# Turning a causal attention's exponentials on VectorE and through DRAM instead of on TensorE

## The chip, the core and the metric

The kernel runs on one core of a Trainium2 chip. Five engines work beside each other, each through its own instructions in a fixed order, and wait for one another by semaphores: TensorE (PE; its weight loads are listed apart as PEld), VectorE (DVE), ScalarE (ACT), GpSimd (POOL), and SyncE (SP), which here only issues DMA transfers. The metric is the time of one execution on the device in microseconds (us); lower is better. All data is float32.

## The reference

Two decoder layers work on x of shape (8, 128, 512): 8 batches of 128 tokens of 512 features. Each of six sublayers is added to x and followed by a layer norm. Layer 0 has a causal attention, an autocorrelation with a context of the same shape, and a gated sum of low-rank experts. Layer 1 has a causal attention with normalized queries and keys and a slope per head, a cross attention, and a low-rank feed-forward. The change is in the two causal attentions, which have 32 heads of 16 features:

```python
scores = jnp.einsum('bhqd,bhkd->bhqk', q, k) / math.sqrt(hd)
scores = jnp.where(causal, scores, -jnp.inf)
att = jax.nn.softmax(scores, axis=-1)
out = jnp.einsum('bhqk,bhkd->bhqd', att, v)
return out.transpose(0, 2, 1, 3).reshape(b, l, d) @ Wo.T + bo
```

Layer 1 clips queries, keys and values to ±8, normalizes queries and keys over all 512 features, and adds slope x (k − q) to the scores before the softmax.

## The kernel before

**A step.** Both attentions go through `Heads16`, which treats 16 pairs of (head, half of the partitions) at once; one such round is called a step. Layer 0 has 16 steps: four pairs of batches (p), and for each four groups of eight heads (f), where the two units of a step are the two batches of the pair. Layer 1 has 16 steps too: eight batches (b), each with f = 0 and f = 2, where the two units are two groups of eight heads. The loops are at lines 516 to 547 and 847 to 897.

A causal mask lets the first 64 queries see only the first 64 keys. So scores are held in two parts: late queries by 128 keys (part 0, two heads x), and early queries by 64 keys (part 1). A step's exponentials are 128 partitions (64 queries of each unit) by 4 rows r by 384 columns.

**What a step does.** The constructor (lines 158 to 187) makes the scores on PE into two pairs of PSUM banks, then on DVE adds the mask or the slopes and takes the minimum of the negated sums, 16 pieces in all (L184), into the tile `e`, which has two buffers. `exps` (L197) makes the exponentials on ACT in place, with their sums. `turn` (lines 213 to 238) transposes `e` on PE, twelve 128x128 blocks into PSUM (L228), since the product with the values needs keys on the partitions; DVE copies the first half to `pT` and ACT the second (L229). `out` multiplies with the values on PE (lines 240 to 257).

The division by the sums differs. In layer 1 `divide` (lines 202 to 211) takes reciprocals on DVE and multiplies the exponentials on POOL, two instructions for each half, before the turn. In layer 0 the reciprocals are spread over 16 features on POOL (L221), turned on PE by two more transposes (L236) and multiplied to the output (L261).

**Order.** In the step n after its scores: the first half of the exponentials, `out` of step n−2, the next step's queries and keys (layer 0) or the next batch's (layer 1), `turn` of step n−1, the second half of the exponentials, and a projection of an earlier pair or batch. Beside layer 0's steps 7 to 15 run pieces of the autocorrelation of the first four batches (`beside`, lines 498 to 508), with much work on DVE in `chosen` (lines 427 to 451).

In layer 1 the queries of batch b+1 are made and normalized in batch b's first step (`normed`, lines 656 to 677; the normalization itself is L667 on DVE), transposed on PE in its second step (`turned_queries`, L691). The keys are normalized in the second step between the two halves of the scores (`between`, lines 174 to 177), transposed (L701) and multiplied with two masks on DVE (L703). The residual's layer norm is made a step later by `catch_up` (lines 117 to 121).

The order in which each engine gets its instructions is not the order of the program text alone. A planner takes them by their place in the text and by when it reckons that their inputs are there, then fixes one list for each engine. `tc.issue_after(x)` holds the instructions inside it behind instruction x on x's engine. A tile of a pool with k buffers waits until the user of the same buffer k tiles before is done. SP's DMA transfers are such a list too: one that waits holds those behind it.

## Time and profile before

| | us |
|---|---|
| median of three runs (lowest to highest) | 883.1 (881.8 to 883.6) |
| the profiled execution | 883.9 |
| its span, first to last instruction | 882.1 |
| layer 0, steps 8 to 14 (91.3 to 198.3 of the span) | 107.0 |
| layer 1, steps 16 to 19 (322.7 to 371.6) | 48.9 |
| layer 1, steps 20 to 29 (371.6 to 481.9) | 110.3 |
| layer 1, from the scores of step 30 to the last projection's end (481.9 to 510.5) | 28.6 |

Layer 0's steps 8 to 14 take 12.4, 16.2, 17.0, 15.8, 12.4, 16.3 and 16.9 us. A batch of layer 1 in its steady part takes 22.1 us.

How to read the profile's lines: a line of a group gives the line of the kernel, the engine, the operation, the output and input tiles, the count, then busy time and the mean of one instruction in ns, and then how long the engine stood idle just before them and what ended that. A line of the DMA issues gives count, size of one and the median time from issue to landing. In the chain of work that ended last each piece has its start, the time that it holds on the chain, and the engine, tile and line. The granted clock of PE is 0.994 of full over the span.

### The profile page before, as it was taken

The page shows a single profiled execution, that of the slowest core. Times are in us where ns is not written, and L with a number is a line of the kernel's source. Part 1 is how long each engine was busy: PE and PEld are TensorE (multiplying, and loading weights), DVE is VectorE, ACT ScalarE, POOL GpSimd, SP SyncE. Part 2 cuts the span into 40 slices and gives each one's busy share as a digit, 9 for nine tenths or more (in the row PEclk, how much of TensorE's full clock was granted, in tenths as well). Part 3 has the DMA queues.
Part 4 walks back from the last instruction along what each step waited for, and adds up shares of the span by engine and source line. Part 5 has one row for each costly group of instructions (what it writes and reads, how often), then busy time and mean ns, then how long its engine had stood idle before and what let it go on. Part 6 is the DMA issues. An engine that isn't in the chain of part 4 may idle for free.

```text
span 882.1 us, 17898 instructions
## 1 busy us (share of the span) xinstructions
PE 853.1 (97%) x6482; PEld 529.9 (60%) x6482; DVE 545.8 (62%) x2166; ACT 369.3 (42%) x1535; POOL 188.5 (21%) x267
## 2 busy tenths in 40 slices
PE   9999999999899999999999999999999999999996
PEld 5766655655455455555555687758475846576454
DVE  3656787777869567777778622735363545467654
ACT  3877564754222136666666503213122322224310
POOL 2500223133333314555555300000000000000000
PEclk9999999999999999999999999999999999999999
DMA  8700000130300002000004010331213211313340
GB/s 327 306 2 26 1 14 13 49 108 1 144 13 24 1 1 97 2 1 2 2 2 145 27 72 1 75 88 42 48 37 85 44 47 37 83 43 76 81 97 36
DMA packets 30073, 50.73 MB, mean 58 GB/s; under 512 B 5536, under 2 KB 22048, under 8 KB 28192
## 3 DMA queue, kind: packets, MB, share of 16 engines
q1 hardware_dynamic: 27424, 47.49, 17.9%
q10 hardware_dynamic: 2560, 2.10, 1.1%
q8 instruction: 51, 0.84, 0.4%
q14 instruction: 38, 0.31, 0.1%
HBM read 30.69 MB, written 2.10 MB: 37 GB/s over the span
## 4 chain that ended last, share of the span: by engine, by line
PE 72%; DVE 17%; ACT 6%; POOL 2%; issue 1%; DMA 1%; SPq 0%; ACTq 0%; POOLq 0%; DVEq 0%
PE pqx L86 9%; PE pox L994 7%; PE pv L86 5%; PE pkx L86 4%; PE pvx L86 4%; PE s_x L932 4%; PE o_x L977 4%; PE pq L86 4%; PE pk L86 3%; PE po L711 3%; ACT e_a L197 3%; DVE e_a L184 3%; PE pt_a L228 3%; PE pof L618 2%; PE s_a L165 2%; PE po L86 2%
## 5 line engine op out<-in xcount | busy, mean ns | idle before, releaser
L197 ACT ACTIVATE e_a<-e_a,m_a 128x128 f32<-128x128 f32 (+1 forms) x512 | 184.8, 365 | 100.2 <-DVE m_a L184 100.2
L953 ACT ACTIVATE e_x<-s_x,m_x 128x256 f32<-128x256 f32 x128 | 58.6, 483 | 140.0 <-DVE m_x L943 132.1
L197 ACT ACTIVATION_READ_ACCUMULATOR e_a<-e_a,m_a 128x1 f32 x512 | 97.6, 191 | 0.0
L86 PE MATMUL pqx<-xTx,w_X_q 128*128 128x256 f32 x384 | 84.9, 380 | 0.0
L86 PEld LDWEIGHTS pqx<-xTx,w_X_q 128*128 128x128 f32 x384 | 72.6, 190 | 11.4 <-issue 1.8
L994 PE MATMUL pox<-w_X_o,oTx 128*128 128x512 f32 x168 | 74.1, 596 | 0.7 <-DVE oTx L983 0.6
L942 DVE TENSOR_REDUCE m_x<-s_x 128x4 f32<-128x1024 f32 x32 | 37.6, 1218 | 41.2 <-PE s_x L932 41.2
L97 POOL TENSOR_TENSOR rs_x<-ve_x,neghalf 128x1 f32<-128x1 f32 x7 | 3.8, 548 | 268.8 <-DVE ve_x L95 249.8
L211 POOL TENSOR_TENSOR e_a<-e_a,rc_a 128x512 f32<-128x512 f32 (+1 forms) x64 | 52.7, 845 | 34.9 <-DVE rc_a L208 19.3
L994 PEld LDWEIGHTS pox<-w_X_o,oTx 128*128 128x128 f32 x168 | 31.3, 190 | 40.9 <-issue 39.2
L932 PE MATMUL s_x<-kTx,qTx 32*128 32x256 f32 x768 | 50.0, 385 | 1.2 <-ACT e_x L953 1.1
L228 PE MATMUL pt_a<-ident,e_a 128*128 128x128 f32 x384 | 48.0, 273 | 2.7 <-DVE m_a L184 2.7
L228 PEld LDWEIGHTS pt_a<-ident,e_a 128*128 128x128 f32 x384 | 43.6, 140 | 11.1 <-issue 5.0
L184 DVE CUSTOM_DVE_ANT_0 e_a<-s_a,masks 128x128 f32<-128x128 f32 (+1 forms) x256 | 47.1, 252 | 4.5 <-PE s_a L165 3.2
L932 PEld LDWEIGHTS s_x<-kTx,qTx 32*128 32x128 f32 x768 | 39.0, 184 | 17.4 <-issue 11.7
L184 DVE CUSTOM_DVE_ANT_0 e_a<-s_a,alibi 128x128 f32<-128x128 f32 (+1 forms) x256 | 47.4, 253 | 2.2 <-PE s_a L165 1.3
L977 PE MATMUL o_x<-pT_x,vx 128*32 128x512 f32 x384 | 43.7, 595 | 1.9 <-issue 0.7
L184 DVE DVE_READ_ACCUMULATOR2_ANT m_a<- 128x1 f32 x512 | 42.4, 83 | 0.1
L961 DVE STREAM_TRANSPOSE e_x<-e_x 128x1024 f32<-128x1024 f32 x32 | 39.7, 1241 | 0.8
L960 DVE TENSOR_SCALAR e_x<-e_x,rc_x 128x256 f32<-128x256 f32 x128 | 36.3, 347 | 3.9 <-DVE rc_x L957 2.2
L165 PEld LDWEIGHTS s_a<-kbd,qT 32*64 32x64 f32 x1024 | 20.7, 131 | 28.5 <-issue 15.4
L103 DVE TENSOR_TENSOR x_x<-pox,x_a 128x512 f32<-128x512 f32 x7 | 4.8, 686 | 52.5 <-PE pox L994 52.5
(236 smaller groups left out, 1627.1 us busy)
## 6 DMA issues: line engine op xcount, KB each, us to landing
pT_x<-e_x SPq DMA_DIRECT2D x224, 64.0 KB, 2.0
w_X_q<-in_X_q SPq DMA_DIRECT2D x3, 1024.0 KB, 4.8
w_X_o<-in_X_o SPq DMA_DIRECT2D x3, 1024.0 KB, 4.7
w_L_Wv<-in_L_Wv SPq DMA_DIRECT2D x2, 1024.0 KB, 7.3
w_L_Wo<-in_L_Wo SPq DMA_DIRECT2D x2, 1024.0 KB, 8.0
x_in<-in_x SPq DMA_DIRECT2D x8, 256.0 KB, 8.5
ct<-in_ctx SPq DMA_DIRECT2D x8, 256.0 KB, 2.6
cT<-in_ctxT SPq DMA_DIRECT2D x4, 512.0 KB, 3.8
```

The lines of the kernel that those rows point to most:

```text
L86: nc.tensor.matmul(ps, lhsT=l, rhs=r, start=(i == 0), stop=(i == n - 1))
L165: nc.tensor.matmul(s[r // 2][64 * u : 64 * u + 64, r % 2, cols], lhsT=qT[rows, 64 - 64 * part : P - 64 * part], rhs=kbd[rows, :, :keys], s ...
L184: self.scored = nc.vector.tensor_tensor_reduce(self.e[:, r, cols], s[i][:, r % 2, cols], bias(r, cols), -1.0, 3e38, ALU.add, ALU.min, self ...
L197: nc.scalar.activation(e[:, r, x, :], e[:, r, x, :], AF.Exp, scale=-1.0, bias=self.m[:, part, r, x : x + 1], accum_out=self.su[:, part, r, ...
L211: nc.gpsimd.tensor_tensor(e, e, bc(self.rc[:, part, rs, :].unsqueeze(3), list(e.shape)), ALU.mult)
L228: nc.tensor.transpose(pt[:, r, cols], self.e[:, 2 * i + r, cols], ident)
L932: nc.tensor.matmul(sc[g // 2][:, g % 2, u * 256 : (u + 1) * 256], lhsT=qT[rows, (h0 + u) * NS + n, :], rhs=kT[rows, n], start=(n == 0), st ...
L942: nc.vector.tensor_reduce(m, self.s[i], AX.X, ALU.max, negate=True)
L953: nc.scalar.activation(self.e[:, :, j, :], self.s[half][:, i, :].rearrange("p (a k) -> p a k", k=32), AF.Exp, bias=self.m[:, j : j + 1], s ...
L961: nc.vector.transpose(self.e[:, :, js, :], self.e[:, :, js, :])
L977: nc.tensor.matmul(po[32 * g : 32 * g + 32, :], lhsT=v[:, s, g * XD + 32 * n : g * XD + 32 * n + 32], rhs=pT[:, s].rearrange("p i h x -> p ...
L994: nc.tensor.matmul(po, lhsT=oT[:, n, h * P : (h + 1) * P], rhs=w, start=(i == 0), stop=(i == NX - 1))
```

## The change

A new class `Squares16` replaces `Heads16` in layer 0's steps 8 to 14 and in layer 1's steps 16 to 30, 22 of 32 steps. It doesn't transpose on PE. Its tile `e` holds four groups of 32 columns apart, with 14 squares of 32 columns in each: twelve of exponentials and two that POOL fills with the reciprocals of the sums. `move` is called in the following step, behind that step's scores on DVE: reciprocals, the copy on POOL, and two DVE transposes, which turn each 32x32 square in place. Then SP stores the whole tile (128 x 1792 floats, 896 KB) to DRAM (`kept`, three buffers) and reads it back by four transfers of 32 partitions each into `pT`, with the squares at the places that a full transposition would give them. The outputs of a step of the new class are made three steps after its scores, with the division by the reciprocals when they are copied out; in layer 1 this replaces the divisions on POOL.

With it go other edits. `pT` has one buffer in layer 0 and two in layer 1; the tiles `rb` and `rT` lie behind `e` and `pT`. Projections come a step later in layer 0's third and fourth pair and a batch later in layer 1; layer 1 has a third buffer for the values and three for `oT`. In layer 1 the queries are normalized on POOL instead of DVE, and the keys' two masked copies are made by two ACT instructions instead of one on DVE. All layer norms left over are made at the end of layer 0's loop.

```diff
@@ -155,8 +155,9 @@
         W = 3 * P
-        def __init__(self, pool, units, bias, o_dst, name, between=()):
+        def __init__(self, pool, units, bias, o_dst, name, between=(), places=1):
             self.pool, self.units, self.o_dst, self.name, self.rc = pool, units, o_dst, name, None
+            self.places = places
             s = [banks(f"s_{name}_{i}") for i in range(2)]
...
-            self.e = pool.tile([P, 4, self.W], F32, tag="e", name=f"e_{name}", bufs=2)
+            self.begin()
-            self.su = sm.tile([P, 2, 4, 2], F32, tag="su_a", name=f"su_{name}")
...
+                                self.head(s[i][:, r % 2], bias, part, r, x)
...
+        def rows(self, tag, bufs):
+            t = self.pool.tile([P, 4 * self.W + self.RB], F32, tag=tag, name=f"{tag}_{self.name}", bufs=bufs)
+            return t[:, : 4 * self.W].rearrange("p (r k) -> p r k", r=4), t[:, 4 * self.W :]
+        def begin(self):
+            self.e, self.behind = self.rows("e", 2)
+            self.su = sm.tile([P, 2, 4, 2], F32, tag="su_a", name=f"su_{self.name}")
...
+        def head(self, s, bias, part, r, x):
+            cols = self.cols(part, x)
+            self.scored = nc.vector.tensor_tensor_reduce(
+                self.block(part, r, x), self.alike(s[:, cols]), self.alike(bias(r, cols)), -1.0, 3e38,
+                ALU.add, ALU.min, self.m[:, part, r, x : x + 1],
+            )
...
+        def move(self, behind):
+            pass
...
-                rb = self.pool.tile([P, 2, 8, HD], F32, tag="rb", name=f"rb_{self.name}", bufs=1)
+                rb = self.behind.rearrange("p (a h d) -> p a h d", a=2, h=8)
                 nc.gpsimd.tensor_copy(rb, bc(rc.rearrange("p (a h) -> p a h", a=2).unsqueeze(3), [P, 2, 8, HD]))
-            self.pT = self.pool.tile([P, 4, self.W], F32, tag="pT", name=f"pT_{self.name}", bufs=1)
+            self.pT, behind = self.rows("pT", self.places)
...
-            self.rT = self.pool.tile([P, 2, P], F32, tag="rT", name=f"rT_{self.name}", bufs=1)
+            self.rT = behind.rearrange("p (a q) -> p a q", a=2)
             nc.scalar.copy(self.rT, pr[:, : 2 * P].rearrange("p (a q) -> p a q", a=2))
+        def probabilities(self, r, t, u):
+            return self.pT[:, r, t * P + 64 * u : t * P + 64 * u + 64]
...
+            self.divided(o)
+        def divided(self, o):
...
+    class Squares16(Heads16):
+        def begin(self):
+            self.tile = self.pool.tile([P, 4, 14, 32], F32, tag="e", name=f"e_{self.name}", bufs=2)
+            self.e = self.tile[:, :, :12, :].rearrange("p g (r t) k -> p r t g k", r=4)
+            self.sums = sm.tile([P, 4, 2, 2], F32, tag="su_a", name=f"su_{self.name}")
+            self.su = self.sums.rearrange("p r a x -> p a r x")
+        def block(self, part, r, x):
+            return self.e[:, r, 2, 2 * x : 2 * x + 2, :] if part else self.e[:, r, x]
+        def alike(self, t):
+            return t.rearrange("p (g k) -> p g k", k=32)
+        def move(self, behind):
+            rc = sm.tile([P, 16], F32, tag="rc", name=f"rc_{self.name}")
+            with tc.issue_after(behind.ins):
+                nc.vector.reciprocal(rc, self.sums.rearrange("p r a x -> p (r a x)"))
+                nc.gpsimd.tensor_copy(
+                    self.tile[:, :, 12:14, :].rearrange("p g a (x d) -> p g (a x) d", x=2),
+                    bc(rc.rearrange("p (r h) -> p r h", r=4).unsqueeze(3), [P, 4, 4, HD]),
+                )
+                for rows in (slice(0, 12), slice(12, 14)):
+                    nc.vector.transpose(self.tile[:, :, rows, :], self.tile[:, :, rows, :])
+            kept = kept_rows.tile([P, 4, 14 * 32], F32, tag="kept", name=f"kept_{self.name}")
+            nc.sync.dma_start(kept, self.tile.rearrange("p g r k -> p g (r k)"))
+            self.pT = self.pool.tile([P, 4, 14, 32], F32, tag="pT", name=f"pT_{self.name}", bufs=self.places)
+            by_group = kept.rearrange("(i k) g x -> k i g x", i=4)
+            to = self.pT.rearrange("p i r k -> p i (r k)")
+            for g in range(4):
+                nc.sync.dma_start(to[32 * g : 32 * g + 32], by_group[:, :, g, :])
+        def turn(self):
+            pass
+        def divide(self, half, behind=None):
+            pass
+        def probabilities(self, r, t, u):
+            return self.pT[:, 2 * u : 2 * u + 2, 3 * r + t, :]
+        def divided(self, o):
+            by_half = "p u (a i q) -> p a u i q"
+            rT = self.pT[:, :, 12:14, :].rearrange("p (u i) a q -> p a u i q", u=2)
+            nc.vector.tensor_tensor(
+                self.o_dst.rearrange(by_half, a=2, i=2),
+                o[:, : 2 * P].rearrange("p (u t) -> p u t", u=2).rearrange(by_half, a=2, i=2),
+                rT[:, ::-1],
+                ALU.mult,
+            )
+    kept_rows = ctx.enter_context(tc.tile_pool(name="kept", bufs=3, space=bass.MemoryType.DRAM))
...
@@ -508,7 +599,8 @@
             piece()
     oTs = []
-    turned = prev = None
+    prev, pending = None, []
+    squares_from = begun + 1
     values_at = {0: [(0, 0), (0, 1)], 2: [(1, 0)], 4: [(1, 1)]}
     for p in range(2, NP):
         values_at[NC * p - 1], values_at[NC * p] = [(p, 0)], [(p, 1)]
@@ -522,12 +614,15 @@
             toks = slice(j * P, (j + 1) * P)
             of = lambda i, w, p=p, f=f, j=j: vs[p, j][i].rearrange("p a x d -> p (a x d)")[:, f * w : (f + 1) * w]
             units.append((qT[:, toks], kbd[:, :, toks], lambda of=of: of(0, 192), lambda of=of: of(1, 128)))
-        now = Heads16(ap, units, causal_bias, oTs[p][:, :, f, :], f"a0_{p}_{f}")
+        by_squares = squares_from <= n < len(steps) - 1
+        now = (Squares16 if by_squares else Heads16)(ap, units, causal_bias, oTs[p][:, :, f, :], f"a0_{p}_{f}")
         now.exps(0)
         catch_up(now.scored)
-        if turned:
-            turned.out()
+        if prev:
+            prev.move(now.scored)
+        while pending and pending[0][0] <= n:
+            pending.pop(0)[1].out()
         if n + 1 < len(steps):
             qk = queries_keys(*steps[n + 1])
         if prev:
@@ -537,23 +632,28 @@
         for made in values_at.get(n, ()):
             values(*made)
         now.exps(1)
-        if 0 < f < 3 and p:
-            projection(2 * p - 3 + f, oTs[p - 1])
+        j = f - 1 - (n - f > squares_from)
+        if 0 <= j < 2 and p:
+            projection(2 * p - 2 + j, oTs[p - 1])
...
-        turned, prev = prev, now
+        pending.append((n + 2 + by_squares, now))
+        prev = now
     assert not beside
+    catch_up()
...
+    outs = [heads.out for _, heads in pending]
     transposed(xs[0], NC, P, fp_tokens[0], "xTf0_0", "a")
-    turned.out()
+    outs[0]()
     transposed(xs[1], NC, P, fp_tokens[1], "xTf0_1", "a")
     prev.turn()
     autos_of[2].spectra()
-    prev.out()
+    outs[1]()
+    outs[2]()
     for j in range(2):
         projection(B - 2 + j, oTs[NP - 1])
...
-    v_bufs = [values_tiles(qp, i) for i in range(2)]
+    v_bufs = [values_tiles(qp, i) for i in range(3)]
...
-            done = nc.vector.tensor_scalar(q, q, mean, rs, ALU.subtract, ALU.mult)
+            done = (nc.vector if i else nc.gpsimd).tensor_scalar(q, q, mean, rs, ALU.subtract, ALU.mult)
...
-        v, vd = v_bufs[b % 2]
+        v, vd = v_bufs[b % 3]
...
-        turned_keys.done = nc.vector.tensor_tensor(kbd, bc(pt.unsqueeze(1), [P, 2, D]), bc(pair.unsqueeze(2), [P, 2, D]), ALU.mult)
+        for x in range(2):
+            nc.scalar.mul(kbd[:, x, :], pt, pair[:, x : x + 1])
         return kbd
@@ -842,26 +943,28 @@
                 self.pieces.pop(0)()
     front = Front(0)
-    turned = prev = oT_before = None
-    keys_late = []
+    prev, pending, oTs, keys_late = None, [], {}, []
     for b in range(B):
         qT, kbd = qk
         v_now = v
-        oT = ap.tile([P, NC, P], F32, tag="oT", name=f"oT1_{b}")
+        oTs[b] = oT = ap.tile([P, NC, P], F32, tag="oT", name=f"oT1_{b}", bufs=3)
         for f in (0, 2):
             units = []
             for i in (f, f + 1):
                 feats = slice(i * P, (i + 1) * P)
                 units.append((qT[:, i, :], kbd[:, :, feats], v_now[0][:, i * 192 : (i + 1) * 192], v_now[1][:, i * 128 : (i + 1) * 128]))
-            now = Heads16(ap, units, alibi_bias(f), oT[:, f : f + 2, :], f"a1_{b}_{f}", keys_late)
+            kind = Heads16 if (b, f) == (B - 1, 2) else Squares16
+            now = kind(ap, units, alibi_bias(f), oT[:, f : f + 2, :], f"a1_{b}_{f}", keys_late, places=2)
             if f == 2 and b + 1 < B:
                 qT = turned_queries(b + 1, raw[0])
             now.exps(0)
             catch_up(now.scored)
-            if turned:
-                turned.out()
+            if prev:
+                prev.move(now.scored)
+            if len(pending) == 3:
+                pending.pop(0).out()
             if b + 1 < B:
                 if f == 0:
                     raw = [normed(0, b + 1, xT)]
@@ -873,12 +976,9 @@
                 E7 = turned_gates(B - 1, routes[B - 1][1]), shared_expert(B - 1, *routes[B - 1])[1]
             if b == B - 1:
                 front.go(1)
-            if prev:
-                prev.turn()
-            now.divide(0, moments.done if f == 0 and b + 1 < B else None)
+            now.divide(0)
             now.exps(1)
-            half = projection(b - 1, oT_before) if f == 2 and b else iter((0, 0))
+            half = projection(b - 2, oTs.pop(b - 2)) if f == 2 and b > 1 else iter((0, 0))
             next(half)
             if b + 1 < B:
                 if f == 0:
@@ -889,17 +989,19 @@
                         chosen_experts(B - 1, *E7, late)
                     with tc.issue_after(chosen_experts.done.ins) if b == 0 else nullcontext():
                         qk = qT, turned_keys(b + 1, raw[1])
-            now.divide(1, turned_keys.done if f == 2 and b + 1 < B else None)
+            now.divide(1)
             if b == B - 1:
                 front.go(1)
             next(half)
-            turned, prev = prev, now
-        oT_before = oT
-    turned.out()
+            pending.append(now)
+            prev = now
+    pending[0].out()
+    list(projection(B - 2, oTs[B - 2]))
     prev.turn()
+    pending[1].out()
     front.go(1)
     prev.out()
-    list(projection(B - 1, oT))
+    list(projection(B - 1, oTs[B - 1]))
     catch_up()
     layer.close()
     for k in ("q0", "q1", "q2"):
```

## The prediction

> **What bounds the kernel now.** I read the page from the top (busy shares, costliest groups, DMA issues), then busy time by stretches, then the chain of work that ended last, cut to the steps the change touches. A step is one round of a causal attention; n counts 0 to 15 in layer 0 and 16 to 31 in layer 1. TensorE (PE) is busy nearly throughout, and the change takes work off it:
>
> ```profile
> span 882.1 us, 17898 instructions
> PE 853.1 (97%) x6482; PEld 529.9 (60%) x6482; DVE 545.8 (62%) x2166; ACT 369.3 (42%) x1535; POOL 188.5 (21%) x267
> ...
> L228 PE MATMUL pt_a<-ident,e_a 128*128 128x128 f32 x384 | 48.0, 273 | 2.7 <-DVE m_a L184 2.7
> ...
> L961 DVE STREAM_TRANSPOSE e_x<-e_x 128x1024 f32<-128x1024 f32 x32 | 39.7, 1241 | 0.8
> ```
>
> A busy PE doesn't mean that it sets every stretch. In the stretches of layer 0's steps 9 and 10 (columns: length, then busy us of PE, weight loads, DVE, ACT, POOL), step 9 has DVE at 15.4 of 16.2 us, while step 10 is PE's:
>
> ```profile
> 103.70:119.90 16.20, 14.76 (x134) 9.03 (x134) 15.41 (x86) 10.51 (x40) 5.30 (x7) 1.00 0.05 18
> 119.90:136.90 17.00, 16.72 (x139) 10.39 (x140) 12.60 (x49) 9.24 (x38) 5.04 (x6) 1.00 0.06 16
> ```
>
> In layer 1 a batch is two steps and 22.14 us. Its chain crosses engines (columns: start, us on the chain, what):
>
> ```profile
> 422.70 0.86 DVE pT_a L229
> 423.56 0.60 DVE st_q L91
> 424.17 0.10 DVE rc_a L208
> 424.27 0.12 DVE mv_q L93
> ...
> 424.41 1.04 POOL e_a L211
> 425.45 0.52 POOL rs_q L97
> ...
> 425.99 1.27 DVE q L667
> ...
> 427.31 0.66 PE pTq L691 x4
> ```
>
> From the scores of a batch's first step (416.75) to the normalized queries (427.26) the chain runs on DVE and POOL, 10.5 us; from there on PE, back to the next batch's scores. So of a batch's two turns (the twelve transposes at L228) only the second step's is on the path. Prices for the new transfers:
>
> ```profile
> w_X_q<-in_X_q SPq DMA_DIRECT2D x3, 1024.0 KB, 4.8
> ...
> w_L_Wo<-in_L_Wo SPq DMA_DIRECT2D x2, 1024.0 KB, 8.0
> ...
> ct<-in_ctx SPq DMA_DIRECT2D x8, 256.0 KB, 2.6
> ...
> out<-x_f SPq DMA_DIRECT2D x7, 256.0 KB, 2.2
> ```
>
> **What it removes.** 22 turns: seven in layer 0 (n = 8 to 14, made in steps 9 to 15), fifteen in layer 1. On the chain twelve transposes take 1.31 us and layer 0's two for the reciprocals 0.22. With them go the copies out of PSUM (DVE 0.95, ACT 0.78) and in layer 1 POOL's four divisions (52.7 us over 16 steps, 3.3 a step). If PE set everything, the gain would be 7 x 1.53 + 15 x 1.31 = 30.4 us.
>
> **What it adds.** DVE transposes of 1536 and 256 elements: L961 takes 1241 ns for 1024; at 1.05 ns an element plus 0.16 us they are 1.78 and 0.43, together 2.2. The reciprocal (0.25) is new only in layer 1, where it replaces two of 0.2. POOL's copy of the reciprocals is L221's 0.40 and lies beside the first transpose. So DVE has +1.26 a step in layer 0. In layer 1 a batch has +4.4 for transposes, −1.9 copies, −0.3 reciprocals, −1.22 (the keys' product L703 goes to ACT), −1.27 (the queries' normalization goes to POOL): about 0, at 17.5 of 22.2.
>
> The transfer is 128 x 7168 B = 896 KB out and again in. I price the store between the 256 KB store (2.2) and 1 MB loads that were alone (4.8) or among others (8.0): from 256 KB to 1 MB the lone loads grow by 2.2 us, so 640 KB more than 256 add 1.8 to the store's 2.2. That is 4.0, by a load's slope; I take 4.4, halfway to the lone 1 MB load, whose rows of 8 KB are nearest to these of 7. Ends: 2.2 and 8.0. The four reads cost SP 0.3 to 0.6 each to issue (16 transfers of pT_x are issued 0.64 apart) and land about 4.7 us after the first.
>
> [...]
>
> [...]
>
> **The new wait: a score tile for two steps.** Tile e has two buffers. Step n's buffer is free only when its store has landed, the store follows its transposes, and these follow the scores of n+1 on DVE. So scores of n+2 stand in DVE's queue behind: scores of n+1 (2.94; 3.30 in a second step, with the keys' normalization between), reciprocal and transposes 2.45, SP's wait 0.15 (L961's end to its first DMA), store 4.4, wake-up 0.05. That is 10.35 for a second step and 10.0 for a first one, or 10.9 where the residual's moments (0.9) go first: 21.2 a batch. Behind a waiting score stand all later DVE work, the exponentials on ACT and, through the normalized queries, PE.
>
> **The queries' path.** From 22.14: −0.86 copy, −0.10 reciprocal, −1.04 division, −1.31 turn, −0.22 (POOL's normalization at 1.05, like a 128x512 product with a broadcast, L450's 1039 ns; its ends are 0.55, as the DVE form alone, and 1.28, L377), +2.45 transposes ahead of it: 21.06. PE alone would need 22.14 − 0.57 − 2.62 = 18.95. I take 21.1, a gain of 1.05 a batch.
>
> **The sum along the path.**
> - Layer 0, turns in steps 10, 11, 12, 14, on PE: 4 x 1.53 = −6.1. Their DVE work has room (12.6 of 17.0, 11.7 of 15.8, 7.4 of 12.4).
> - Steps 9 and 13, on DVE: +1.26 less idle time of 0.8, so +0.5 to +1.3 each; +1.6.
> - Its end: scores of 15 at 198.4, on DVE until 202.2; transposes 204.6, store 209.2, reads 213.9, outputs 214.7, where the last projections started at 212.7: +2.0. Batch 5's projection, one step later, fills this wait on PE.
> - Layer 1, steps 16 to 19: 48.9 before; 14.2, then waits for e of 10.35, 10.9 and 10.35: 45.8, so −3.1.
> - Steps 20 to 29, five batches: −5.3.
> - Its end: projection 6 moves behind the loop (+3.44), two turns go (−2.62), and outputs of 30 wait for scores of 31 (492.4, once e is free) + 2.9 + 2.45 + store and reads 9.2 = 507. Between +1.5 (a piece of the cross attention, 2.58, moves up to fill it) and +4; +2.5.
>
> Sum −8.4. The profiled run took 883.9 (span 882.1 and 1.8 around it): 875.5. The median shown is 0.8 lower; predicted 875.
>
> Taken at nothing: ACT's two products for the keys (1.2 at the copy of 128x512, 0.58 each) lie under the second half of the projection (1.72); behind eight exponentials (2.9) they would cost a batch up to 2.3. Blocks of four runs of 32 in scores, exponentials and output products: L953 writes such runs, 483 ns for 256, against 454 for L357 in one run: 0 to 0.03 each, on engines with room. SP's queue: reads of n in layer 0 wait for outputs of n−1, the next store, tokens and context stand behind them; outputs of n−1 come 2 us into a step, the store 6. Weight loads in layer 1 (five of 1 MB) wait in the same queue for their slot; one placed too early holds a store by up to a step, 10 us. The outputs' distance: a round trip ends about 15.2 us after the scores of n+1, outputs of n stand two steps (21) behind these, so 6 us to spare; were it gone, PE would wait by the excess in each step. The third value buffer and its POOL fills cost nothing that anyone waits for.
>
> **Rivals.**
> 1. PE sets the layers (0.22): the planner, whose order is made anew, puts queries' transposes and moments where nothing waits, and the store lands in about 2.5 to 3.5. For it: 256 KB stores in 2.2, PE's 18.95 a batch. Against: the chain above crosses DVE in every batch. It gives 30 less 5 to 14 for the ends and steps 9 and 13: 853 to 868.
> 2. The store holds e (0.27), slower. Fourteen intervals in layer 1 go through it (scores of 17 to scores of 31). Each us of landing above 4.4 costs them 14 us, so from 5.0 us the whole gain is gone; at 6.0 the time is 897, at 7.3 (w_L_Wv, 1 MB among others) 915. For it: no transfer to DRAM of this size in the trace, five weight loads in the same stretch. Against: the 256 KB store is faster than the load.
> 3. No net change (0.06): the queries' path keeps its 22 us because transposes and POOL's work lie ahead of it, and the ends eat layer 0's gain: 881.5 to 885.
>
> **How the numbers follow.** The forecast (868 to 881.5) has 0.45. About 0.2% (1.8 us) is what a measurement can tell from no change. Faster: 0.45 + 0.22 = 0.67; same 0.06; slower 0.27. Range for 8 in 10: rival 1 down to 857 (its last 4 us left out) and rival 2 up to 891 (landing of 5.5): 857 to 891. The likeliest case alone: 868 to 881.5.
>
> **What would show it.** Right: L228 at 120 instances; DVE's larger transposes near 1.78; a step of layer 1 at 10 to 10.9 us with scores (L184's successor) waiting for the store of kept by some us; steps 10 to 12 shorter by 1.5 each, 9 and 13 not. Wrong: no DVE wait for the store (rival 1), a landing over 5 us (rival 2), PE waiting for pT at the outputs, or a stage beyond 510 us that moves by itself.

## The result, and the profile after

The changed kernel takes 938.1 us (median; 937.3 to 938.6) against 882.4 for the kernel before on the same chip: 1.063 times as long, 95% interval 1.061 to 1.066. The forecast was 875.0, within 857 to 891. The profile's own execution has a span of 936.1 us against 882.1, and 53.6 of these 54 us lie in four stretches, taken between the first score matmuls of the steps named:

| us | before | after | difference | forecast |
|---|---|---|---|---|
| steps 8 to 14 | 107.1 | 109.7 | +2.6 | −4.5 |
| scores of 15 to scores of 16 (layer 0's end and the experts) | 124.4 | 138.9 | +14.5 | +2.0 |
| steps 16 to 30 | 165.8 | 192.2 | +26.4 | −8.4 and part of +2.5 |
| behind the scores of 31 | 393.7 | 403.8 | +10.1 | part of +2.5 |

The page of the changed kernel, as before: span, busy shares, the granted clock in 40 slices, the transposes on VectorE, and the new DMA issues (count, size of one, median us to landing).

```profile
span 936.1 us, 17538 instructions
...
PE 849.2 (91%) x6204; PEld 516.3 (55%) x6204; DVE 546.0 (58%) x2157; ACT 363.3 (39%) x1522; POOL 163.2 (17%) x232
...
PEclk9999999797999999788899899999999999999998
...
L329 DVE STREAM_TRANSPOSE e_a<-e_a 128x1536 f32<-128x1536 f32 (+1 forms) x44 | 45.8, 1073 | 0.0
...
kept_a<-e_a SPq DMA_DIRECT2D x22, 896.0 KB, 4.0
pT_a<-kept_a SPq DMA_DIRECT2D x88, 224.0 KB, 4.3
```

The change does what it says: 278 matmul instructions fewer, 44 transposes on VectorE (1.73 and 0.415 us by form), a store of 4.0. No engine is a new bound: TensorE falls from 97% busy to 91%, all others stay under 60%. So the time went into waits. The waits of the changed kernel (engine, line, what it waited for: us in total, times, longest):

```profile
DVE oT L350 <- PE o_a L280: 57.1, 17, 7.8
...
PE pTq L791 <- POOL q L767: 29.9, 6, 6.9
...
PEld s_a L166 <- ACT kbd L804: 13.4, 7, 4.5
...
PE o_a L274 <- DMA pT_a<-kept_a: 11.6, 3, 7.8
...
PE s_a L166 <- ACT kbd L804: 8.3, 6, 4.3
...
DVE e_a L205 <- DMA kept_a<-e_a: 2.5, 1, 2.5
```

The wait that the prediction was built on, scores for e's store, is the last line: 2.5 us, once. Above it stand four others (the one for the keys' product kbd has two lines, for weight loads and for matmuls). The sum had the first three at nothing, and the wait for the read-back only as a part of layer 0's end. Three of them meet in each batch of layer 1, as the chain of work that ended last shows for one batch (start, us on the chain, what):

```profile
418.42 1.16 ACT kbd L804 x2
...
419.62 0.91 PE s_a L166 x32
...
428.40 0.60 DVE q L763
429.00 0.60 DVE k L763
429.60 0.60 DVE st_q L91
430.20 0.59 DVE st_k L91
...
431.14 0.56 POOL rs_q L97
...
431.79 2.09 POOL q L767
...
433.93 1.12 PE pTq L791 x4
...
436.48 5.09 PE pv L86 x8
441.57 0.45 PE pt_xTa L129 x4
...
442.04 0.59 ACT xTa L139
442.63 2.87 ACT e_a L218 x16
445.50 1.16 ACT kbd L804 x2
```

Read it from the top. The queries' clip (428.40) is followed on VectorE by the keys' clip, and each moment of the queries by one of the keys: some 1.3 us of keys' work on the queries' path. POOL then normalizes for 2.09 us. TensorE, which had made the second step's scores by 429.2, idles 4.7 us until 433.9; the values' products behind that wait take 5.09 us instead of 3.63. VectorE has an output's copy (oT, L350) in its queue ahead of the second step's scores, and that output stands behind pTq on TensorE: the scores, ready at 429.2, begin at 436.9. ACT makes the first eight of their sixteen exponentials by 440.3. Its list then has the next tokens' copy (xTa), for which it waits 1.7 us, since the transposes that it copies (pt_xTa) stand behind the values' products on TensorE. The other eight exponentials (2.87 us; the profile counts each with its sum, so x16) and the keys' two products follow, and the next batch's scores wait 0.8 us for them; over the layer this wait is 8.3 us. So the way from the queries to the next scores leads through the slowed products, not through the late scores. A batch takes 27.2 us, 8.7 for its first step and 18.5 for the second, where it took 22.1.

At layer 0's end the chain runs through a round trip:

```profile
214.96 0.43 DVE oT L350
...
216.72 4.65 DMA pT_a<-kept_a
...
221.61 0.66 PE o_a L274 x16
...
223.18 0.44 DVE oT L350
...
223.64 0.81 ACT pT_a L253
...
224.49 3.54 PE pa L489 x8
```

Step 13's output frees the one buffer of pT, step 14 is read back into it, and only its output frees it for the turn of step 15, which is copied out of the banks that the spectra (pa) want. They start at 224.5; before, at 208.2.

### The profile page after: what moved, and what is told of

It reads as the page before. It is cut to its first block, busy times and chain, and to the rows that moved or that the text cites. A ratio compares the mean times of both kernels' runs of the same rounds, so it can differ in the third digit from the quotient of the medians.

```text
span 936.1 us, 17538 instructions
## 1 busy us (share of the span) xinstructions
PE 849.2 (91%) x6204; PEld 516.3 (55%) x6204; DVE 546.0 (58%) x2157; ACT 363.3 (39%) x1522; POOL 163.2 (17%) x232
## 4 chain that ended last, share of the span: by engine, by line
PE 49%; DVE 11%; ACT 6%; issue 4%; POOL 3%; DMA 2%; SPq 1%; ACTq 1%; POOLq 0%; DVEq 0%
PE pqx L86 9%; PE pox L1096 6%; PE pv L86 4%; PE s_x L1034 4%; PE o_x L1079 4%; PE pvx L86 3%; PE pkx L86 3%; ACT e_a L218 3%; PE pof L718 2%; DVE e_a L205 2%; POOL q L767 1%; PE o_a L274 1%; PE pof L728 1%; PE pox L1323 1%; DMA kept_a<-e_a 1%
## 5 line engine op out<-in xcount | busy, mean ns | idle before, releaser
L1034 PEld LDWEIGHTS s_x<-kTx,qTx 32*128 32x128 f32 x768 | 39.0, 184 | 16.7 <-issue 11.7
L166 PE MATMUL s_a<-kbd,qT 32*64 32x128 f32 (+1 forms) x1024 | 34.2, 344 | 13.0 <-ACT kbd L804 8.3
L329 DVE STREAM_TRANSPOSE e_a<-e_a 128x1536 f32<-128x1536 f32 (+1 forms) x44 | 45.8, 1073 | 0.0
L350 DVE TENSOR_TENSOR oT<-o_a,pT_a 128x256 f32<-128x256 f32 x22 | 9.3, 423 | 62.5 <-PE o_a L280 57.1
L274 PE MATMUL o_a<-pT_a,v 128*32 128x64 f32 x1024 | 30.2, 253 | 11.7 <-DMA pT_a<-kept_a 11.6
L86 PE MATMUL pv<-w_L_Wv,xTa 128*128 128x512 f32 x64 | 38.8, 761 | 0.0
```

The source lines that it names most:

```text
L86: nc.tensor.matmul(ps, lhsT=l, rhs=r, start=(i == 0), stop=(i == n - 1))
L166: nc.tensor.matmul(s[r // 2][64 * u : 64 * u + 64, r % 2, cols], lhsT=qT[rows, 64 - 64 * part : P - 64 * part], rhs=kbd[rows, :, :keys], s ...
L274: nc.tensor.matmul(o[32 * r : 32 * r + 32, late], lhsT=v[:, 48 * r + 16 * x : 48 * r + 16 * x + 32], rhs=self.probabilities(r, x, u), star ...
L329: nc.vector.transpose(self.tile[:, :, rows, :], self.tile[:, :, rows, :])
L1034: nc.tensor.matmul(sc[g // 2][:, g % 2, u * 256 : (u + 1) * 256], lhsT=qT[rows, (h0 + u) * NS + n, :], rhs=kT[rows, n], start=(n == 0), st ...
```

## Experiments

Times are medians; "before" is the kernel before on the same chip, 882.2 to 883.7 in all comparisons.

### Which layer: l0_only and l1_only

The first has the change in layer 0 alone and layer 1's loop as before, the second the other way round:

```diff
-    squares_from = begun + 1
+    squares_from = len(steps)        # l1_only
```

> The change in layer 0 alone; layer 1 is as before. If the two layers' costs add, what the two profiles show up to the scores of step 16 is what it costs: steps 8 to 14 take 109.8 us for 107.0, and from there to the scores of step 16 it is 138.9 for 124.4, so 17 us slower than before (14 to 20). Theory A, the order of the queues: the loss sits in steps 12 and 13, where PE stands behind banks that scores hold, and at the end, where pT's one buffer and the last round trip stand ahead of the spectra (7.8 us). The rival, that layer 1's loss lowers the clock or shifts the order of everything, would have layer 0 alone within 5 us of before.

> The change in layer 1 alone; layer 0 is as before. If the costs add: 26.4 us from the scores of step 16 to those of step 31 and 10.2 behind them, 37 us slower than before (33 to 40). With the run of layer 0 alone the two sums should give the whole, 54 to 56.

Measured: l0_only 902.2, 19.0 above before (ratio 1.022, 1.020 to 1.023); l1_only 920.1, 36.9 above (1.043, 1.041 to 1.045). Together 55.9, as the whole change costs 55.7. The layers can be studied apart.

### The queries' normalization: q_on_dve and before_q_pool

```diff
-            done = (nc.vector if i else nc.gpsimd).tensor_scalar(q, q, mean, rs, ALU.subtract, ALU.mult)
+            done = nc.vector.tensor_scalar(q, q, mean, rs, ALU.subtract, ALU.mult)
```

q_on_dve is the changed kernel with this edit, before_q_pool the kernel before with the opposite one.

> The changed kernel with one edit undone: layer 1's queries are normalized on DVE. Theory A: the queries' transposes on PE wait for POOL's 2.08 us and hold outputs, values and projections behind them in PE's queue; DVE does it in 0.55 now that POOL's divisions are gone, so 1.5 us a batch at least come back, 10 us in seven batches, and up to 28 if PE's clock no longer falls in the wait. Theory B, the store and the round trip (scores wait for e, outputs for pT): layer 1 stays at 27 us a batch, a gain below 3 us.

> The kernel before with that one edit alone: queries normalized on POOL. The chain from scores to queries gets 2.08 us instead of 1.27, behind POOL's divisions: 0.8 to 1.5 us a batch, 6 to 11 us slower. If the edit only hurts together with the squares, within 2 us of before.

Measured: q_on_dve 925.3, 12.8 below the changed kernel, theory A near its lower end; before_q_pool 893.1, 9.9 above before (1.012, 1.010 to 1.015), as expected. One instruction that the prediction took as a gain of 0.22 us a batch costs 12.8 us in the changed kernel and 9.9 in the kernel before. Its groups, by form, in the kernel before (with the keys' like instruction below it), then in before_q_pool, then in q_on_dve:

```profile
L667 DVE TENSOR_SCALAR q<-q,mv_q,rs_q 128x512 f32<-128x512 f32 x8 | 9.3, 1165 | 9.4 <-POOL rs_q L97 9.4
...
L667 DVE TENSOR_SCALAR k<-k,mv_k,rs_k 128x512 f32<-128x512 f32 x8 | 4.3, 544 | 0.7 <-POOL rs_k L97 0.7
```

```profile
L667 POOL TENSOR_SCALAR q<-q,mv_q,rs_q 128x512 f32<-128x512 f32 x8 | 16.6, 2078 | 0.2
```

```profile
L767 DVE TENSOR_SCALAR q<-q,mv_q,rs_q 128x512 f32<-128x512 f32 x8 | 4.4, 546 | 4.5 <-POOL rs_q L97 4.5
```

On POOL it takes 2.08 us in both kernels. On VectorE it took 1.17 on average before. Seven of the eight took 1.25, each beside POOL's divisions over its whole length (the timeline of before has three of these from 425.93 to 428.29); the eighth, and all eight of the keys, ran with POOL idle and took 0.55. With the divisions gone all eight take 0.55. So the change by itself had more than halved the instruction (1.25 to 0.55) that it then moved to an engine where it takes 2.08.

### What else waits in layer 1: qk_on_dve, qk_dve_outs_behind, filled

Each adds to the one before. First the keys' product goes back to VectorE too; then an output's VectorE instruction may be placed only behind the step's scores; then the projection is split, its first half ahead of the queries' transposes, its second half behind the keys':

```diff
-        for x in range(2):
-            nc.scalar.mul(kbd[:, x, :], pt, pair[:, x : x + 1])
+        turned_keys.done = nc.vector.tensor_tensor(kbd, bc(pt.unsqueeze(1), [P, 2, D]), bc(pair.unsqueeze(2), [P, 2, D]), ALU.mult)
...
             if len(pending) == 3:
-                pending.pop(0).out()
+                with tc.issue_after(now.scored.ins):
+                    pending.pop(0).out()
...
+            next(half)
             if f == 2 and b + 1 < B:
-                qT = turned_queries(b + 1, raw[0])
+                with tc.issue_after(projection.done.ins) if b > 1 else nullcontext():
+                    qT = turned_queries(b + 1, raw[0])
```

> The changed kernel with both of its moved instructions of layer 1 back on VectorE: the queries' normalization (as in the run q_on_dve, 925.3 us) and the keys' product kbd (one VectorE instruction of about 1.1 us instead of two on ScalarE behind sixteen exponentials). Theory A (order of the engines' queues): the next batch's scores no longer wait for ScalarE's last exponentials, the PEld wait 's_a <- ACT kbd' is gone, and a batch of layer 1 shortens from 24.4 us to 21 to 22.5: 905 to 916 us. Theory B (the products on ScalarE are covered, the rest of the loss is the round trip through DRAM): a batch stays at 24 to 25.5 and the time at 922 to 930.

> As qk_on_dve, and in layer 1 an output's VectorE instruction (L350, which waits for TensorE) may be placed only behind the score additions of the step beside it. Theory A: the scores of a batch's second step, which TensorE has ready some 8 us before, no longer stand behind an output that waits for TensorE; a further 1 to 3 us of each batch goes, 4 to 15 us below qk_on_dve. Theory B (the outputs' place is without weight, since TensorE is what the second step waits for): within 3 us of qk_on_dve.

> As qk_dve_outs_behind (911.8 us), with the projection of layer 1 split around the transposed queries and keys on TensorE: its first half (1.7 us) ahead of the queries' transposes, for which TensorE waits 2.6 us in each batch, its second half behind the keys' transposes. A batch is 23.3 us there, of which the values' eight products take 4.9 to 5.3 us where they took 3.63 before the change. Theory A (the wait costs twice, by itself and because the products after it run at a lower granted clock): a batch loses 2.5 to 3.5 us in batches 2 to 6, 894 to 900 us, and the values' products come back to 3.6 to 4.2. Theory B (the clock does not depend on that wait): 1.7 us a batch, 903 to 906, the products still above 4.8. Theory C (the scores' wait for e's store takes the wait's place): 907 or more, with VectorE waiting for kept.

Measured, with layer 0's 19 us still in each (batches and products are those of steps 20 to 29):

| | time | a batch (first + second step) | eight products of pv (before: 3.7) |
|---|---|---|---|
| the changed kernel | 938.1 | 27.2 (8.7 + 18.5) | 4.9 to 5.4 |
| q_on_dve | 925.3 | 24.3 (8.7 + 15.6) | 4.0 to 5.5 |
| qk_on_dve | 916.1 | 23.6 (8.7 + 14.9) | 4.3 to 5.3 |
| qk_dve_outs_behind | 911.8 | 23.2 (8.7 + 14.5) | 3.7 to 5.4 |
| filled | 905.7 | 20.9 (8.7 + 12.2) | 3.7 |

Each is a term of layer 1's loss: 12.8, 9.2, 4.3 and 6.1 us. The keys' product lands at the edge of its theory A by time (916), and the outputs' place just inside theirs, but their steady batches gain only 0.7 and 0.4 us, less than theory A had in both. By its time filled fits theory B, but by its batches and products theory A: a batch lost 2.3 us, 11.0 over steps 16 to 30, and of that 4.1 us went again behind the scores of 31 and 2.9 at layer 0's end, whose orders were made anew with it. Theory C fell: VectorE waits for kept 3.8 us in all.

The last column goes with the granted clock. A stretch of layer 1's steady part in the changed kernel, then one in filled (columns: from and to, length, busy us of PE, weight loads, DVE, ACT and POOL, then the granted clock):

```profile
410.00:520.00 110.00, 87.97 (x819) 45.39 (x819) 68.01 (x366) 60.82 (x290) 31.12 (x40) 0.87 0.49 144
```

```profile
397.00:472.00 75.00, 68.75 (x721) 34.43 (x720) 65.50 (x314) 48.29 (x242) 22.18 (x34) 1.00 0.59 176
```

TensorE's wait for the queries and the products behind it, in the changed kernel, in filled and in before_q_pool (start, us, instruction; in brackets the idle time before and what ended it):

```profile
433.93 1.12 PE L791 MATMUL pTq<-ident,q 128*128 128x128 f32 x4 [4.69 <-POOL q L767]
...
436.41 5.16 PE L86 MATMUL pv<-w_L_Wv,xTa 128*128 128x512 f32 x8
```

```profile
421.74 0.63 PE L791 MATMUL pTq<-ident,q 128*128 128x128 f32 x4 [0.80 <-DVE q L767]
...
423.11 3.70 PE L86 MATMUL pv<-w_L_Wv,xTa 128*128 128x512 f32 x8
```

```profile
409.17 0.66 PE L691 MATMUL pTq<-ident,q 128*128 128x128 f32 x4 [2.34 <-POOL q L667]
...
410.56 3.70 PE L86 MATMUL pv<-w_L_Wv,xTa 128*128 128x512 f32 x8
```

In filled TensorE waits 0.8 us for the queries, the clock is 1.00 and the products take 3.7 us in every batch of the steady part. In the changed kernel it waits 4.7 us, the clock is 0.87, and in the trace the first four values' products behind the wait start 0.85 to 1.02 us apart, the last four 0.43. Waits of 2.6 to 3.1 us, in the three kernels between, gave all from 3.7 to 5.5. The kernel before had made a turn there (twelve transposes at 420.99, between the queries' and the keys' products) and waited 0.57 us. before_q_pool, which keeps that turn, waits 2.34 us in each of its five steady batches, and its products stay at 3.7, with a granted clock of 1.00 from 410 to 520 us; so the slow instruction on POOL alone didn't lower the clock there.

In the changed kernel the granted clock, read in stretches of 0.2 us, falls from 1.00 to 0.50 in each of the five steady batches while TensorE waits for the queries (4.2 us in the first, 4.7 in the others), 2.4 to 3.7 us after it fell idle, and is 1.00 again 5.0 to 5.9 us behind the wait's end; the slow products lie in that stretch. The length of the wait alone doesn't tell which products slow: of five waits of 2.6 us in qk_dve_outs_behind four had slowed products behind them (up to 5.4 us for the eight), the fifth not (3.7).

### Layer 1 put in order: l1_best and l1_best2

Layer 0 is as before here, to see whether layer 1 gains at all. l1_best adds to filled that the keys' clip stands behind the queries' moments, and that both steps of the last batch turn on TensorE; l1_best2 that step 29 does so too, and that the last addition of a projection stands behind the last scores:

```diff
+        with tc.issue_after(normed.queries.ins) if i else nullcontext():
             nc.vector.tensor_scalar(q, pq, 8.0, -8.0, ALU.min, ALU.max)
...
-            kind = Heads16 if (b, f) == (B - 1, 2) else Squares16
+            kind = Heads16 if (b, f) >= (B - 2, 2) else Squares16    # l1_best: b == B - 1
...
+            behind = None if f == 0 else turned_keys.on_pe if b + 1 < B else now.scored
+            with tc.issue_after(behind.ins) if behind else nullcontext():
                 next(half)
```

> Layer 0 as in the kernel before; layer 1 as in the run filled, and besides: the keys' clip stands behind the queries' moments on VectorE (they were paired, 1.3 us ahead of the queries), and both steps of the last batch turn on TensorE as before, so that the last round trip does not stand in front of the layer's end. Theory A (all of layer 1's loss is order, and TensorE then sets a batch at 19 to 20.5 us): from step 16's scores to step 31's 148 to 155 us against 165.7 before, the part behind them within 3 us of before's 382.6, the time 868 to 877 us, faster than before (883.2). Theory B (e's store holds the scores, as the prediction had it, at 20.5 to 21.5 a batch): 877 to 883. Theory C (transposes on VectorE cost more than they free): above 883.

> As l1_best (885.9 us), whose batches are shorter than before by 1.4 to 2.1 us but whose part behind step 31's scores is 14.5 us longer than before: there step 31's scores stand on VectorE behind projection 5's addition and norm, which wait for TensorE until 486.6, and e's buffer comes free only with step 29's store. Here the addition is held behind the scores, and step 29 too turns on TensorE. Theory A (these two make the longer end): the part behind step 31's scores loses 8 to 14 us, and the time is 872 to 879, faster than before (883.7). Theory B (the end is longer because its work, batch 6's and 7's projections and outputs, moved behind the loop whatever the order): 882 or more.

Measured: l1_best 885.9 (1.003, 1.002 to 1.004), l1_best2 878.5 (0.9947, 0.9934 to 0.9961). l1_best missed theory A: its steps 16 to 30 take 153.3 us, as theory A had it (its first steady batches take 19.9, those of filled 20.9), but the stretch behind the scores of 31 took 408.2 instead of 393.7. In l1_best2 that stretch is 396.5; its edits were not run apart. This kernel is faster than before by 0.5%, 4.1 us, as its theory A had it. The page of l1_best2, and its waits for the store:

```profile
span 876.5 us, 17696 instructions
...
PE 838.3 (96%) x6326; PEld 514.0 (59%) x6326; DVE 553.9 (63%) x2166; ACT 361.0 (41%) x1522; POOL 151.7 (17%) x230
```

```profile
DVE e_a L205 <- DMA kept_a<-e_a: 7.4, 4, 2.6
```

Most batches take 19.9 us (8.7 + 11.2), and now the store is waited for, 7.4 us in four times: the wait of the prediction is there once the others are gone. That the turning itself makes the 4.1 us is not shown: the kernel before was not run with its projection split in the same way, and TensorE waits 4.8 us there for the queries in all.

### Where layer 0 loses: l0_to_11, l0_pieces_behind

Both start from l0_only. The first stops with step 11:

```diff
-        by_squares = squares_from <= n < len(steps) - 1
+        by_squares = squares_from <= n < len(steps) - 4
```

The second holds the autocorrelation's first pieces of a step on TensorE behind the next step's queries and keys. In the changed kernel the planner had put a product of theirs (pvf, L551) ahead of them in step 13, where it waits 5.1 us for banks that hold scores.

```diff
+        with tc.issue_after(queries_keys.done.ins):
             auto(n, 0)
```

> The change in layer 0 alone, and there only for steps 8 to 11; steps 12 to 15 and layer 1 are as in the kernel before (l0_only: 902.2 us, of which steps 8 to 11 gained 3.7 against before, 12 to 14 lost 6.4 and the layer's end lost 14.5). Theory A (the loss is that the last round trips stand before the layer's end with one buffer for the turned exponentials, and the planner's order in steps 12 to 14): the end is as before, 123 to 126 us from step 15's scores to step 16's, and the time is 877 to 885 us. Theory B (wherever the squares stop, the steps that follow pay for the outputs that are still to come): 890 to 902 us.

> l0_only with the first pieces of the auto-correlation of each step (among them L551, for which TensorE waits 5.1 us in step 13) placed behind the next step's queries and keys on TensorE. If it is their place in TensorE's queue that makes steps 12 to 14 longer than before (14.1, 18.9, 19.0 us against 12.4, 16.2, 17.0), those steps lose 3 to 6 us and the time is 895 to 900 us; if it is the round trip or VectorE's own work, within 2 us of l0_only's 902.2, or above it.

Measured: l0_to_11 896.3, theory B's time, and l0_pieces_behind 902.9, no gain. Stopping earlier moves the loss: l0_to_11's end is nearly back (128.5), but step 13 takes 28.7 us instead of 16.2, since there, too, a turn on TensorE follows the last round trip through the one buffer. Its chain in step 13, where the outputs of 10 free the buffer for the reads of 11, and the outputs of 11 for the turn of 12:

```profile
173.96 0.42 DVE oT L350
...
175.70 4.74 DMA pT_a<-kept_a
...
180.57 0.43 PE o_a L274 x16
...
181.51 0.44 DVE oT L350
181.97 0.81 ACT pT_a L253
```

Placing the pieces behind shortens steps 12 and 13 from 14.1 and 18.9 to 10.9 and 17.1, and the end takes it back (143.0 instead of 139.3): what sets the end is not when step 15 starts.

### The end of layer 0, link by link: l0_13_apart, l0_15_apart, l0_15_apart_pieces, l0_out13_ahead, l0_copy_first

The buffer was my theory. l0_13_apart reads step 13 back into a free weight buffer, l0_15_apart puts the last turn's pT there instead:

```diff
-            self.pT, behind = self.rows("pT", self.places)
+            w = wp.tile([P, 2048], F32, tag="w", name=f"pT_{self.name}")     # step 15 alone
+            self.pT = w[:, : 4 * self.W].rearrange("p (r k) -> p r k", r=4)
```

> l0_only (902.2 us) with one edit: the turned exponentials of step 13 are read back into a free weight buffer instead of the one buffer for pT, so that the reads of step 13 need not wait for the outputs of step 12, nor those of step 14 for the outputs of step 13. In l0_only the last outputs go one behind the other through that buffer: outputs of 13, reads of 14 (4.7 us and more), outputs of 14, the turn of 15, and the spectra (pa) start some 15 us later than before. Theory A (this row of two round trips is what layer 0's end loses): the reads of 13 and 14 overlap, pa starts 6 to 9 us earlier than in l0_only, from step 15's scores to step 16's it is 130 to 133 us against 139.3, and the time is 893 to 897. Theory B (the end loses by the order of the queues or by VectorE's work, not by the buffer): within 2 us of 902.

> l0_only (902.2 us) with the turned exponentials of step 15, the last one and turned on TensorE, in a free weight buffer of their own, so that this turn and the spectra behind it no longer wait until step 14's outputs have freed the one pT buffer (in l0_only TensorE idles 7.7 us there, and the spectra start at 224.2 against 208.2 before). Theory A (the last round trip stands before the spectra through that buffer): the spectra start 7 to 11 us earlier, the last projections follow the outputs of step 14 (222 to 225 instead of 230), step 15 to 16 takes 130 to 134 us instead of 139.3, the time is 893 to 898. Theory B (the outputs of step 14 hold the end anyway, through the projections): 900 to 903.

> As l0_15_apart, and the autocorrelation's first pieces of each step behind the next step's queries and keys on TensorE, as in l0_pieces_behind, where steps 12 and 13 took 4 us less but the end took them back (902.9). Theory A (there the last round trip hid what the steps gained): now they count, 889 to 894. Theory B (what the steps gain is lost again behind them): within 2 us of l0_15_apart.

Measured: 901.9, 902.0 and 898.5. l0_13_apart: theory A fell. Of two trips in a row the first had cost little: in l0_only step 14's store is issued at 209.2 and lands at 213.7, and its reads, which then wait for the buffer, are issued at 215.2. The last trip by itself stands before the spectra. l0_15_apart has theory B's time: counted from step 15's scores, the spectra start at 10.6 us instead of l0_only's 23.1, but the last projections at 36.0 instead of 29.1. l0_15_apart_pieces has the spectra where they were before the change (207.9), as theory A wanted, and still gains only 3.7 on l0_only, between its two theories: the planner now puts the outputs of 13 behind the autocorrelation's last products, the reads of 14 start at 224.7, and the last projections at 233.5. l0_out13_ahead mends this:

```diff
+    with tc.issue_after(pending[0][1].made.ins):      # outputs of 13
         autos_of[2].correlate()
```

> As l0_15_apart_pieces (898.5 us), with the autocorrelation's last products (pc) behind the outputs of step 13 on TensorE. Theory A (what layer 0's end loses is the last round trip in front of the last projections, however it is arranged, and its start is set by when the buffer before it comes free): outputs of 13 at 214 to 216 instead of 221.8, reads of 14 land at 220 to 223 instead of 230.7, the last projections at 222 to 226 instead of 233.5, the time 888 to 893, still above before. Theory B (the end is set by something else, VectorE's work in the autocorrelation): 896 or more.

Measured: 899.1, theory B's number, though step 14's reads land at 223.0 as theory A had it. TensorE's timeline (start, us, instruction, and in brackets the idle time before and what ended it):

```profile
223.01 0.43 PE L280 MATMUL o_a<-pT_a,v 128*32 128x64 f32 x16 [2.13 <-DMA pT_a<-kept_a]
...
224.76 3.36 PE L86 MATMUL po<-w_L_Wo,oT 128*128 128x512 f32 x4
233.15 7.71 PE L86 MATMUL po<-w_L_Wo,oT 128*128 128x512 f32 x12 [5.04 <-DVE oT L356]
```

The outputs are made at 223 to 225, but VectorE's list has their copies behind the autocorrelation's search, until 232.7. l0_copy_first holds the search behind them:

```diff
+    with tc.issue_after(pending[-1][1].copied.ins):   # outputs of 15
         third.chosen(0)
```

> As l0_out13_ahead (899.1 us), with the autocorrelation's search on VectorE behind the copies of step 14's and 15's outputs. Theory A (the end loses by what stands behind the late outputs in each queue, the round trip itself costing what it does not hide): the last projections start at 224 to 227 instead of 233.2, the search 3 us later than there, step 15 to 16 at 130 to 135 us against 140.1 and 124.4 before, the time 890 to 895. Theory B (the search is the end's own chain, so that what the projections gain it loses): 896 to 900.

Measured: 889.9 (1.0078, 1.0059 to 1.0097), theory A. The last projections start at 226.1, and the end takes 133.0 instead of 139.3. Of layer 0's 19.0 us 7.7 are left: steps 8 to 14 are at 104.9, below before, and the end is still 8.6 above it. The end in the kernel before and in l0_copy_first (columns as above):

```profile
198.31:322.66 124.35, 118.91 (x612) 63.69 (x611) 88.62 (x316) 34.53 (x92) 39.14 (x54) 0.99 0.09 32
```

```profile
198.88:331.90 133.02, 123.19 (x654) 65.03 (x653) 90.53 (x324) 33.90 (x90) 40.75 (x56) 0.99 0.22 73
```

TensorE has 42 matmuls more there than before, since work has moved into this stretch from the steps: the 48 of one step's outputs and eight of batch 5's projection, less one turn's fourteen. That is 4.3 us of busy time, and one reason why the steps are shorter. The other 4.4 us are idle time, of which 3.3 is the wait for step 14's reads.

### Both layers: best_both, best_both2

l1_best2 with layer 0 as in l0_15_apart_pieces, and as in l0_out13_ahead.

> Both layers changed: layer 0 as in l0_15_apart_pieces, layer 1 as in l1_best2 (878.5 us with layer 0 as before, 4.1 below before). The parts added up so far within 1 us, so by theory A 885 to 890, by theory B of the run above 890 to 896; faster than l1_best2 only if layer 0's change gains by itself, which no run has shown.

> best_both (888.4 us) with the same edit. By theory A 877 to 883, at best level with l1_best2 (878.5), whose layer 0 is as before; by theory B 886 or more.

Measured: 888.4 and 889.6 (both 1.007): theory A for best_both, theory B for best_both2. Layer 0's change takes back more than layer 1's gains. Of all kernels here only l1_best2 beats the kernel before. l0_copy_first's edit was not run with l1_best2; if the parts add, 7.7 lost and 4.1 gained leave that pair slower than before too, by an estimate of 3.6 us.

## Why the prediction was wrong

**The operations were priced right, but for POOL's normalization.** The turns went (L228's successor has 120 instances); transposes 1.73 and 0.415 against 1.78 and 0.43; the store 4.0 against 4.4. Rival 2, a slow store, is out, though the 0.27 for slower stood on it alone; so is rival 1 as the change stands.

**"The queries' path", −0.22 for POOL's normalization: failed.** It costs +0.82 (2.09 for 1.27), above the upper end that I gave (1.28), because I took a product with a broadcast as its nearest row. And the row of 1.27 was itself swollen by POOL's divisions, which the change removes: left in place it would have been −0.7.

**The same path had no term for its queue.** I summed what an instruction takes, and not what the new order puts before it: the keys' clip and moments among those of the queries (1.3 us; in the kernel before they come at 427.17, behind the queries' normalization at 425.99), and the output's copy ahead of the second step's scores. I had named the planner's new order in rival 1 as a gain; as a loss I had named only a weight load placed too early in SP's queue.

**"Taken at nothing: ACT's two products": failed.** They don't lie under the second half of the projection. On the chain they stand behind eight exponentials, the case that I had priced at up to 2.3 a batch and then left out. The next scores wait for them, 8.3 us in all, and with qk_on_dve 9.2 us went.

**PE's clock had no term.** The transposes that I took off for "PE alone would need 18.95" had kept TensorE at work in the queries' wait. Without them it idles there (4.7 us where it was 0.57), and behind the wait, at a granted clock of 0.50, the first values' products start 0.85 to 1.02 us apart instead of 0.43: the eight alone take 1.5 us a batch more. Layer 0 has it too, with a granted clock of 0.92 over steps 8 to 14 (before 1.00) and 0.94 over the end (0.99). In the end it costs little: 654 matmuls are busy for 123.7 us at 0.94 in the changed kernel, and as many for 123.2 at 0.99 in l0_copy_first. PE's busy time fell by 3.9 us in all, not by some 30.

**The wait for e's store, 21.2 a batch: not what ended last.** It came once, for 2.5 us. Instead of −3.1 steps 16 to 19 changed by +2.6, and instead of −5.3 steps 20 to 29 by +25.1. With the order repaired these stretches come out close to the forecast: 46.0 in l1_best2 (forecast 45.8) and 103.1 (105.0). That is partly luck: most batches take 19.9 and one 23.7, and l1_best2's order isn't the one that was priced.

**Layer 1's end, +2.5: failed, at 8.7** (from the scores of 30 on; 4.7 in l1_best2, where two steps more turn on TensorE). By the expectation of l1_best2 the last scores stood behind projection 5's addition and e's last store; its edits together took 11.7 us off the stretch behind the scores of 31. Which of them did it stays open.

**Layer 0's steps: failed.** Instead of −1.5 each in steps 10, 11, 12 and 14 they changed by −2.1, +0.2, +1.7 and +2.0, and steps 9 and 13 by −1.8 and +2.7. The order was new in the later ones (step 13's wait at pvf); with the pieces placed behind and step 15's buffer apart, the seven steps took 106.2 us, and 104.9 with the two later edits: 0.9 and 2.2 less than before, of the 4.5 that I forecast.

**Layer 0's end, +2.0: failed, at 14.5.** I let the outputs come at 214.7 and had batch 5's projection fill the wait. I hadn't asked what stands behind the outputs: the one buffer, the turn of step 15, the spectra, then the search on VectorE. Batch 5's projection did run before the read-back (at 204.9), and yet TensorE waited for it.

## What to carry to other kernels

When work leaves a bound engine, look at what it had been covering: here the freed TensorE idled in the same waits (4.7 us for 0.57), and the eight products behind them took 4.9 to 5.4 us instead of 3.7. When an edit removes an instruction's neighbour, price the instruction anew before moving it (1.25 us before, 0.55 without POOL's divisions). A transfer that is hidden in a loop's steady state can be bare at its last pass, as the 4.65 us of step 14's read-back were, so count every list that the last pass's result stands in, link by link.

## What the runs showed of the hardware

A normalization of 128x512 floats with two per-partition scalars takes 0.55 us on VectorE with POOL idle, 1.25 beside POOL's products of two inputs (seven of eight in the kernel before), and 2.08 on POOL. A store of 896 KB to DRAM lands in 4.0 us (the median of 22 in the changed kernel), less than one of the four transfers that read a quarter of it back (4.3). After idling 4.2 to 4.7 us in the changed kernel's steady batches TensorE had a granted clock of 0.50, for another 5.0 to 5.9 us from the wait's end; the eight products of pv there took 4.9 to 5.4 us instead of 3.7. After 2.6 us they took more than 3.7 in four of five batches (qk_dve_outs_behind), after 2.34 in none of five (before_q_pool).
